# The last stage of layer 0 with residual sums made by accumulating transfers, a pinned instruction order, and first neighbours taken from the chip

## Chip, cores and metric

One core of one Trainium2 chip runs the whole program. The metric is device microseconds of one execution, median of several runs. The engines are named as the profile names them: PE (TensorE), DVE (VectorE), ACT (ScalarE), POOL (GpSimd), SP (SyncE, which here only issues transfers).

## What is computed

Four graph layers over x of shape (8, 2048, 64), with an adjacency of 2048 x 2048. The change touches the end of layer 0 and the start of layer 1:

```python
# layer 0: industry = (adj/deg) @ (h W_ind); g = hypergraph attention
def attn_scores(f):
    return jnp.tanh(f @ fcW + fcb) @ av
pair   = jnp.stack([industry, g], axis=2)
coefs2 = jax.nn.softmax(attn_scores(pair), axis=-1)
out    = jnp.einsum('bnk,bnkf->bnf', coefs2, pair)
x = x + out
# layer 1
h = jnp.maximum(_layernorm(x), 0.0) @ W
e = leaky_relu(s_src[:, :, None] + s_dst[:, None, :], 0.2)
x = x + elu(softmax(where(adj > 0.5, e, -inf)) @ h)
```

A softmax over two entries is a sigmoid of the difference of the scores, and sigmoid(d) is (1 + tanh(d/2))/2. So with c = tanh((s_ind - s_g)/2) the layer adds g + 0.5 (1 + c)(industry - g) to x.

## The kernel before

Two of the eight batches sit side by side on the 128 partitions (64 features each), so there are NP = 4 pairs p. The 2048 nodes of a pair are cut into NCW = 4 pieces c of CW = 512 columns. A chunk is one (p, c), a tile of 128 x 512 fp32 or 256 KB; there are 16.

Layer 0 first computes `industry` and writes it to DRAM (`ind_dram`, line 947), then g, which stays on the chip in `gT` (four tiles of 128 x 2048, the same memory as `hn`; last written by line 1165). Then comes the stage that the change rewrites, lines 1193 to 1264. For each chunk:

- `front` (1211): load `iv` from `ind_dram` on SP; `scores` twice, for `iv` and for the columns of `gT`: two matmuls with `fcW` into `pf` (1206) and one tanh of 128 x 1024 on ACT into `th_s` (1208); on DVE the difference of the two `th_s` (1217) and `iv - gv` (1218).
- `back` (1221): two matmuls with `Av` into `pd` (1224), tanh on ACT into `cc` (1226), and three DVE operations (1227, 1228, 1229) that end in x + out; the tile goes to `x1_dram` by a transfer that POOL issues (1230).
- `inputs` (1232): x of the chunk, `xo`, is loaded on SP into one of five buffers.

`back` runs two chunks behind `front`. After the last chunk of a pair, `late_tile` (1827) loads 1 MB of the adjacency over `gT[p]`, from POOL's queue.

Between chunks the generator `neighbour_steps(0)` of layer 1 (1288) is advanced, from the eighth chunk on: for each c it loads x1 of pair 0 back from `x1_dram` (1302), takes the layer norm (`mean`, `var`, Square, Ln, Exp: lines 730 to 741), and multiplies by `W1x` into `ph` (1319), from which `vd`, `sc` and `hS` are made (1320 to 1322). At its end it makes `wd` and `rs` (1328, 1330), transposes `rs` and writes it to `r_dram` (1337). For the first half of pair 0, the broadcast rows R are built on the chip: 8 small matmuls into `pb` (1345) and 4 ACT copies (1346).

Then `attend` of layer 1 starts: for each of 16 tiles m, DVE makes two `pt` (1387) from R, `wd` and the adjacency, and PE multiplies them into `o` and `dn`. This loop is PE's from then on.

The order of instructions on an engine is chosen by a scheduler except where `keep_in_program_order` pins it; in this stage only every second matmul of a pair is pinned (1198). A transfer waits in its issuing engine's queue (SP or POOL) until what it needs is there, and everything behind it in that queue waits too. Transfers issued by SP run on the queue that the profile calls q1, those issued by POOL on q0.

Of the kernel before, what the change touches and what calls it, by code (L numbers as in the profile page):

```python
# [8 lines left out]
FP = mybir.dt.float32  # L9
FR = mybir.dt.float32r  # L10
AF = mybir.ActivationFunctionType
OP = mybir.AluOpType
# [4 lines left out]
P = 128  # L17
# [601 lines left out]
LN_EXP = "natural_log_exp_and_others"  # L619


class Kit:


# [124 lines left out]
def layer0(kit, hn, x1_dram, open_early, late_tile, between):  # L749
# [40 lines left out]
    with ExitStack() as sA:  # L790
# [110 lines left out]
        with ExitStack() as s1:  # L901
# [11 lines left out]
            def industry(c):  # L913

                acc = [ps.tile([P, CW], FP, tag=f"acc{p}", name=f"acc{p}") for p in range(NP)]
                ds = sb.tile([P, 2, CW], FR, tag="ds", name="ds")
                for g in range(NT // 2):
                    at = sp.tile([P, 2, CW], FR, tag="at", name="at")
                    nc.gpsimd.dma_start(
                        out=at,  # L920
                        in_=t["adjT"][g * 2 * P : (g + 1) * 2 * P, cols(c)].bitcast(FR).rearrange("(k p) n -> p k n", p=P),
                    )
                    for k in range(2):
                        m = 2 * g + k
                        for p in range(NP):
                            for h in range(2):
                                mm(acc[p], Y[h][:, m, p, :], at[:, k, :], start=m + h == 0, stop=m == NT - 1 and h == 1)  # L927
                        if units:
                            units.pop(0)()

                    if g > 0:
                        nc.vector.tensor_tensor(ds, (was if g == 1 else ds).bitcast(FP), at.bitcast(FP), op=OP.add)
                    was = at
                ev = [sb.tile([P, CW], FP, tag="ev", name="ev", bufs=4) for p in range(NP)]
                for p in range(NP):
                    (nc.scalar.copy if p % 2 else nc.vector.tensor_copy)(ev[p], acc[p])  # L936
                deg = ps.tile([P, CW], FP, tag="ph", name="deg", bufs=2)
                for k in range(2):
                    mm(deg, ones_r, ds[:, k, :], start=k == 0, stop=k == 1)
                rdeg = sb.tile([P, CW], FP, tag="rdeg", name="rdeg", bufs=1)  # L940
                nc.vector.tensor_reduce(bad[:, 3 + c : 4 + c], deg, AX.X, OP.min)
                nc.vector.tensor_scalar(bad[:, 3 + c : 4 + c], bad[:, 3 + c : 4 + c], 0.5, None, op0=OP.is_lt)
                nc.vector.tensor_scalar_max(rdeg, deg, 1.0)
                nc.vector.reciprocal(rdeg, rdeg)
                for p in range(NP):
                    nc.vector.tensor_mul(ev[p], ev[p], rdeg)
                    nc.sync.dma_start(out=ind_dram[p, :, cols(c)], in_=ev[p])
# [152 lines left out]
    with ExitStack() as s0:  # L1100
# [64 lines left out]
                nc.scalar.activation(gT[p][:, i * P : (i + 1) * P], pt[:, p, :], AF.Identity, bias=neg1)  # L1165

        now = begin(0)
        late = None
        for i in range(NT):
            pg = ps.tile([P, B, F], FP, tag="pg", name="pgs")  # L1170
# [16 lines left out]
        late()  # L1187

    sP.close()
    next_ = between(None)  # L1190


    with ExitStack() as s0:
        io = s0.enter_context(tc.tile_pool(name="o_io", bufs=7, reuse_waits="tile"))
        sb = s0.enter_context(tc.tile_pool(name="o_sb", bufs=2, reuse_waits="tile"))
        ps = s0.enter_context(tc.tile_pool(name="o_ps", bufs=2, space=PSUM, reuse_waits="tile"))

        def pinned(ins, first):

            if not first:  # L1200
                tc.keep_in_program_order(ins)

        def scores(v):
            pf = ps.tile([P, 2, CW], FP, tag="pf", name="pf")
            for b2 in range(2):
                pinned(mm(pf[:, b2, :], fcW[half(b2), :], v[half(b2), :], start=True, stop=True), b2 == 0)
            th = sb.tile([P, 2, CW], FP, tag="th", name="th_s", bufs=4)
            nc.scalar.activation(th, pf, AF.Tanh, bias=fcb)
            return th

        def front(p, c):
            s = cols(c)
            iv = io.tile([P, CW], FP, tag="iv", name="iv")
            nc.sync.dma_start(out=iv, in_=ind_dram[p, :, s])
            gv = gT[p][:, s]
            th = [scores(iv), scores(gv)]
            nc.vector.tensor_sub(th[0], th[0], th[1])
            nc.vector.tensor_sub(iv, iv, gv)
            return p, s, gv, th[0], iv

        def back(x, p, s, gv, th, df):
            pd = ps.tile([P, CW], FP, tag="pd", name="pd")
            for b2 in range(2):
                pinned(mm(pd[half(b2), :], Av, th[:, b2], start=True, stop=True), b2 == 0)
            cc = sb.tile([P, CW], FP, tag="cc", name="cc", bufs=1)
            nc.scalar.activation(cc, pd, AF.Tanh, scale=0.5)
            nc.vector.scalar_tensor_tensor(df, cc, 1.0, df, op0=OP.add, op1=OP.mult)
            nc.vector.scalar_tensor_tensor(df, df, 0.5, gv, op0=OP.mult, op1=OP.add)
            nc.vector.tensor_add(x, x, df)
            nc.gpsimd.dma_start(out=x1_dram[p, :, s], in_=x)  # L1230

        def inputs(p, c):
            x = sb.tile([P, CW], FP, tag="x", name="xo", bufs=5)
            nc.sync.dma_start(out=x, in_=t["xT"][p, :, cols(c)])
            return x

        behind, freed, xs = [], [], []

        def finish():
            p, c, rest = behind.pop(0)  # L1240
            back(xs.pop(0), *rest)
            if freed:
                late_tile(freed.pop())
            if c == NCW - 1:
                freed.append(p)

        for p in range(NP):
            for c in range(NCW):
                behind.append((p, c, front(p, c)))
                if len(behind) > 1:  # L1250
                    xs.append(inputs(*behind[-2][0:2]))

                if NCW + 2 < p * NCW + c:
                    next(next_, None)
                if len(behind) > 2:
                    finish()
                if NCW + 2 < p * NCW + c:
                    next(next_, None)
        xs.append(inputs(*behind[-1][0:2]))
        for _ in next_:  # L1260
            pass
        while behind:
            finish()
        late_tile(freed.pop())
    ctx.close()


class Layer1:
# [19 lines left out]
    def neighbour_steps(self, p):  # L1288
# [3 lines left out]
        nc, mm = kit.nc, kit.mm  # L1292
        x1_dram, r_dram = self.x1_dram, self.r_dram

        keep = self.sb2 if p else sb
        sc = sb.tile([P, NT, 4], FP, tag="sc", name="sc", bufs=1)
        vd = keep.tile([P, NT, 2], FP, tag="vd", name="vd", bufs=1 + (p > 0))
        wd = keep.tile([P, NT, 2], FP, tag="wd", name="wd", bufs=1 + (p > 0))
        hS = None
        for c in range(NCW):  # L1300
            x = sb.tile([P, CW], FP, tag="x", name="x1", bufs=1)
# [27 lines left out]
        rs = sb.tile([P, 2, NT], FP, tag="rs", name="rs", bufs=1)  # L1329
        nc.scalar.activation(rs, sc[:, :, 2:4].rearrange("p t b -> p b t"), AF.Exp, scale=-0.8)  # L1330
        pr = ps.tile([2 * NT, P], FP, tag="h", name="pr")
        one = nc.tensor.transpose(pr, rs.rearrange("p b t -> p (b t)"), kit.ident)
        if kit.strict:
            kit.tc.keep_in_program_order(one)
        rr = sb.tile([2 * NT, P], FP, tag="rr", name="rr", bufs=1)
        nc.vector.tensor_copy(rr, pr)
        nc.sync.dma_start(out=r_dram[p].rearrange("b (t n) -> (b t) n", n=P), in_=rr)
        self.first = [self.scores(p, 0, b2) for b2 in range(2)] if p == 0 else None

        for b2, r in enumerate(self.first or ()):  # L1340
            for k in range(2):
                pb = ps.tile([P, 4, P], FP, tag=("ln", "h")[k], name="pb1")
                for j in range(4):
                    one = rs[:, b2, 4 * k + j : 4 * k + j + 1]
                    mm(pb[:, j, :], one.to_broadcast([P, P]), kit.ident, start=True, stop=True)
                nc.scalar.copy(r[:, cols(k)], pb.rearrange("p k n -> p (k n)"))
        yield hS, vd, wd

    def scores(self, p, hf, b2):

        self.turn += 1
        r = (self.sb2 if self.turn % 3 == 0 else self.R).tile([P, HN], FP, tag="R", name="R", bufs=2 - (self.turn % 3 == 0))
        if p == hf == 0:
            return r
        self.kit.nc.sync.dma_start(out=r, in_=self.r_dram[p, b2 : b2 + 1, cols(hf, HN)].to_broadcast([P, HN]))
        return r

# [57 lines left out]

        return [lambda: total(0), end]

    def run(self, aT, now, following):

# [4 lines left out]
        self.ps2 = l1.enter_context(tc.tile_pool(name="att_ps", bufs=2, space=PSUM, reuse_waits="tile"))  # L1426
        kit.use_ln_exp()
        kit.strict = True
        ends = []
        for p in range(NP):  # L1430
            last = p == NP - 1
            if last:
# [362 lines left out]
def four_layers(  # L1795
# [13 lines left out]
    with ExitStack() as s:  # L1809
# [18 lines left out]
            load(NT - NP + p, low.tile([P, N], FR, tag=f"hn{p}", name=f"aTl{p}"))  # L1828

        def between(_):  # L1830
            one = Layer1(kit, x1)
            ahead.append(one)

            def steps():
                for r in one.neighbour_steps(0):
                    yield
                ahead.append(r)

            return steps()

        layer0(kit, hn, x1, early, late_tile, between)
        later = []
# [2 lines left out]
            later.append(Layers23(kit, x1, x3, out, part, ctx))  # L1845
            return later[0].front(ps)

        ahead[0].run(aT, ahead[1], following)
        later[0].run(aT)
        ps = s.enter_context(tc.tile_pool(name="flag_ps", bufs=1, space=PSUM))  # L1850
        nc.vector.tensor_reduce(kit.bad[:, 0:1], kit.bad, AX.X, OP.add)
# [47 lines left out]
```

## Time and profile before

| what | us |
|---|---|
| runs before, median (lowest to highest) | 2101.84 (2101.09 to 2102.75) |
| the profiled execution, its own time | 2095.15 |
| its span | 2093.3 |
| last transposes of g (line 1163) start | 436.14 |
| first matmul of the stage (line 1206) | 437.16 |
| `wd`, `rs` on ACT | 523.36 to 523.73 |
| first two `pt` of layer 1 start on DVE | 532.94 and 534.15 |
| first `o` matmul | 534.27 |

The stage takes 97 us, from 437 to 534, a twentieth of the span; the 1560 us after it are bound by PE and the change does not touch their instructions. A line of the timeline reads: start, duration, engine, line, operation, output<-inputs, shapes, count; the bracket is the idle time before it and what ended it. In a chain of waits each row is start, duration, and what the end was waiting for in that time.

### The profile page before, as it was taken

How to read it: one execution, taken by the hardware profiler on the slowest of the kernel's cores; microseconds unless marked ns; L12 is line 12 of the kernel's file. 1: busy time of each engine (PE TensorE's matmuls, PEld its weight loads, DVE VectorE, ACT ScalarE, POOL GpSimd, SP SyncE). 2: the span in 40 equal slices, each digit the busy share in tenths (PEclk: the TensorE clock that was granted, in tenths of full speed). 3: DMA queues.
4: the chain of work that ended last, by engine and by line, in shares of the span. 5: the costliest groups of instructions: out<-in, count | busy, mean ns of one | idle time of the engine just before them, and what ended most of it. 6: DMA issues, size and time to landing. Idle time of an engine off the chain costs nothing.

```text
span 2093.3 us, 23652 instructions
## 1 busy us (share of the span) xinstructions
PE 2017.3 (96%) x9164; PEld 1153.1 (55%) x9164; DVE 1211.8 (58%) x1906; ACT 461.6 (22%) x863; POOL 260.1 (12%) x384
## 2 busy tenths in 40 slices
PE   7999998988999999999999999999999999999997
PEld 4777655622332223226776457765477755577653
DVE  6677388876888888884223652226642246522355
ACT  4321244456211111112121111211111211112100
POOL 0211054420000000000001120002110012100022
PEclk9999899998999999999999999999999999999999
DMA  5666272145211111213210112101022001121000
GB/s 128 184 193 194 81 254 53 37 138 163 63 40 43 39 44 23 61 31 81 59 46 16 28 28 66 56 11 31 22 59 62 30 21 25 37 66 56 6 16 12
DMA packets 85001, 136.06 MB, mean 65 GB/s; under 512 B 32912, under 2 KB 33168, under 8 KB 82640
## 3 DMA queue, kind: packets, MB, share of 16 engines
q1 hardware_dynamic: 66832, 83.86, 13.8%
q0 software_dynamic: 18048, 50.60, 8.8%
q8 instruction: 74, 1.21, 0.2%
q14 instruction: 47, 0.39, 0.1%
HBM read 103.69 MB, written 30.74 MB: 64 GB/s over the span
## 4 chain that ended last, share of the span: by engine, by line
PE 68%; issue 15%; DVE 6%; POOL 5%; DMA 3%; ACT 2%; POOLq 0%; SPq 0%; DVEq 0%; ACTq 0%
PE acc L713 27%; PE o L713 11%; PE dn L713 6%; PE u L713 6%; PE acc L927 2%; PE pgs L1155 2%; PE var L713 2%; PE mean L713 2%; PE py L713 2%; POOL fold L1780 1%; DVE ex L1153 1%; PE ph L713 1%; POOL ot L1781 1%; DMA at<-in_adjT 1%; POOL mix L1154 1%
## 5 line engine op out<-in xcount | busy, mean ns | idle before, releaser
L713 PE MATMUL acc<-aT,parts 128*128 128x512 f32 x1664 | 456.0, 420 | 0.0
L713 PEld LDWEIGHTS acc<-aT,parts 128*128 128x128 f32 x1664 | 307.8, 188 | 111.8 <-issue 49.4
L1768 DVE TENSOR_TENSOR pr<-u,embf 128x512 f32<-128x512 f32 x256 | 170.5, 686 | 139.0 <-PE u L713 132.3
L1387 DVE SCALAR_TENSOR_TENSOR pt<-R,wd,aT 128x1024 f32<-128x1024 f32 x192 | 236.6, 1277 | 22.2 <-PE dn L713 8.4
L713 PE MATMUL o<-pt,hS 128*64 128x512 f32 x1024 | 239.4, 604 | 6.5 <-DVE pt L1387 6.5
L713 PE MATMUL u<-W3f,y 64*128 64x512 f32 x1024 | 241.0, 589 | 0.0
L713 PEld LDWEIGHTS u<-W3f,y 64*128 64x128 f32 x1024 | 99.2, 187 | 120.6 <-issue 120.6
L713 PEld LDWEIGHTS o<-pt,hS 128*64 128x64 f32 x1024 | 68.7, 137 | 166.9 <-issue 151.3
L713 PE MATMUL u<-W3f,v 64*128 64x512 f32 x512 | 138.8, 619 | 0.0
L927 PE MATMUL acc<-at,Y 128*128 128x512 f32 x512 | 134.8, 408 | 1.5 <-DVE ev L936 1.5
L713 PE MATMUL dn<-pt,vd 128*32 128x512 f32 x1024 | 123.1, 598 | 0.0
L1604 DVE TENSOR_TENSOR yb<-py,cb_f 128x512 f32<-128x512 f32 x32 | 22.1, 691 | 173.8 <-PE py L713 173.8
L1780 POOL TENSOR_TENSOR fold<-fold 128x256 f32<-128x256 f32 x64 | 47.7, 746 | 548.5 <-DVE fold L1779 510.6
L927 PEld LDWEIGHTS acc<-at,Y 128*128 128x128 f32 x512 | 93.9, 191 | 24.5 <-issue 4.3
L713 PE MATMUL acc<-aTl,parts 128*128 128x512 f32 x384 | 103.1, 405 | 0.0
L1772 DVE TENSOR_TENSOR pr<-pr 128x512 f32<-128x512 f32 x128 | 88.0, 688 | 2.2
L1387 DVE SCALAR_TENSOR_TENSOR pt<-R,wd,aTl 128x1024 f32<-128x1024 f32 x64 | 79.7, 1281 | 11.5 <-PE dn L713 8.2
L713 PEld LDWEIGHTS acc<-aTl,parts 128*128 128x128 f32 x384 | 72.2, 188 | 21.5 <-issue 5.7
L1155 PE MATMUL pgs<-mix,S 128*128 128x512 f32 x128 | 69.7, 635 | 12.8 <-POOL mix L1154 12.0
L1754 ACT COPY xs<-px 128x128 f32<-128x128 f32 x64 | 17.1, 267 | 272.7 <-POOL ot L1782 210.2
L1154 POOL TENSOR_TENSOR mix<-ex,wt 128x512 f32<-128x512 f32 x64 | 66.6, 1042 | 74.1 <-DVE ex L1153 65.0
L1672 POOL TENSOR_TENSOR bq<-bq,xp 128x512 f32<-128x512 f32 x16 | 20.5, 1282 | 434.1 <-DVE xp L1670 395.6
(307 smaller groups left out, 2709.1 us busy)
## 6 DMA issues: line engine op xcount, KB each, us to landing
at<-in_adjT POOLq DMA_DIRECT2D x32, 512.0 KB, 4.6
raw<-in_adjT SPq DMA_DIRECT2D x64, 256.0 KB, 3.3
aT<-in_adjT POOLq DMA_DIRECT2D x12, 1024.0 KB, 5.9
xp<-xd SPq DMA_DIRECT2D x45, 256.0 KB, 2.9
R<-r_dram SPq DMA_DIRECT2D x14, 512.0 KB, 3.9
hi_dram<-hi SPq DMA_DIRECT2D x16, 264.0 KB, 2.5
lo_dram<-lo SPq DMA_DIRECT2D x16, 264.0 KB, 3.4
hhi<-hi_dram POOLq DMA_DIRECT2D x16, 264.0 KB, 3.0
```

Source lines behind the costliest of these rows:

```text
L713: one = self.nc.tensor.matmul(*args, **kw)
L927: mm(acc[p], Y[h][:, m, p, :], at[:, k, :], start=m + h == 0, stop=m == NT - 1 and h == 1)
L1153: nc.vector.scalar_tensor_tensor(ex, mix, 1.0, ex, op0=OP.max, op1=OP.min)
L1154: nc.gpsimd.tensor_tensor(mix, ex, wt[:, k, :, None].to_broadcast([P, B, F]), op=OP.mult)
L1155: return lambda: mm(flat(pg), S[:, k, :], flat(mix), start=k == 0, stop=k == NB - 1)
L1387: nc.vector.scalar_tensor_tensor(pt, R[b2], wd[:, m, b2 : b2 + 1], aT[m][:, s].bitcast(FP), op0=OP.max, op1=OP.mult)
L1604: nc.vector.tensor_tensor(yb, py, bias[:, None, :].to_broadcast([P, 4, P]), op=OP.add)
L1672: nc.gpsimd.tensor_add(bq, bq, xp)
L1768: nc.vector.tensor_tensor(a, u[h], emb[:, i, 8 * w : 8 * w + 8, None].to_broadcast([P, 8, F]), op=OP.mult)
L1772: nc.vector.tensor_add(pr[h], pr[h], a)
L1780: nc.gpsimd.tensor_add(fold[:, :, 0:2, :], fold[:, :, 0:2, :], fold[:, :, 2:4, :])
L1781: nc.gpsimd.tensor_add(ot, fold[:, :, 0, :], fold[:, :, 1, :])
```

## The change

The stage becomes a software pipeline in a fixed order: all its matmuls, ACT and DVE instructions are pinned (`InOrder` wraps an engine and pins all that it issues). At step i the engines get `first(i+1)` (load, scores of industry), `second(i+1)` (scores of g, and `iv - gv/2`), `third(i-1)` (`pd` and its tanh, now written in place in PSUM), `differ(i)` and `fourth(i-2)`.

The arithmetic is rearranged. `ind_dram` now holds half of industry (the reciprocal of twice the degree), and the tanh of its scores has scale 2. `fourth` makes df = (1 + c)(ind/2 - g/2) in one operation. What is left, x + g + df, is summed differently by pair: for pair 0 on DVE, with x loaded into four tiles `xs` that stay on the chip; for pairs 1 to 3 in DRAM: x is copied there from the input early (three transfers of 1 MB, DRAM to DRAM, issued by SP), `gT[p]` is added to it by a transfer with `accum_op=add` (1 MB each, POOL), and each chunk's df by another (256 KB each, POOL).

`first_neighbours` replaces `neighbour_steps(0)`: it works on two pieces at a time, straight from `xs`, and is advanced twice a step from step 4 on. R of the first half is now loaded from `r_dram` (two transfers of 512 KB) and no longer built from `pb`.

```diff
-                nc.vector.tensor_scalar_max(rdeg, deg, 1.0)
+                nc.vector.tensor_scalar(rdeg, deg, 1.0, 2.0, op0=OP.max, op1=OP.mult)
...
         now = begin(0)
+        for p in range(1, NP):
+            nc.sync.dma_start(out=x1_dram[p], in_=t["xT"][p])
...
+    V, A = InOrder(tc, nc.vector), InOrder(tc, nc.scalar)
+        io = s0.enter_context(tc.tile_pool(name="o_io", bufs=9, reuse_waits="tile"))
...
+        def first(i):
+            p, c = chunks[i]
+            iv = ivs[i] = io.tile([P, CW], FP, tag="iv", name="iv")
+            nc.sync.dma_start(out=iv, in_=ind_dram[p, :, cols(c)])
+            ths[i] = scores(iv, 2.0)
+        def second(i):
+            p, c = chunks[i]
+            tgs[i] = scores(gT[p][:, cols(c)], 1.0)
+            V.scalar_tensor_tensor(ivs[i], gT[p][:, cols(c)], -0.5, ivs[i], op0=OP.mult, op1=OP.add)
+        def differ(i):
+            V.tensor_sub(ths[i], ths[i], tgs.pop(i))
+        def third(i):
+            pd = ps.tile([P, CW], FP, tag="pd", name="pd")
+            th = ths.pop(i)
+            for b2 in range(2):
+                mm(pd[half(b2), :], Av, th[:, b2], start=True, stop=True)
+            A.activation(pd, pd, AF.Tanh, scale=0.5)
+            ccs[i] = pd
+        def fourth(i):
+            p, c = chunks[i]
+            df = ivs.pop(i)
+            V.scalar_tensor_tensor(df, ccs.pop(i), 1.0, df, op0=OP.add, op1=OP.mult)
+            if p:
+                nc.gpsimd.dma_start(out=x1_dram[p, :, cols(c)], in_=df, accum_op=OP.add)
+            else:
+                V.tensor_add(df, df, gT[p][:, cols(c)])
+                V.tensor_add(xs[c], xs[c], df)
+                nc.sync.dma_start(out=x1_dram[p, :, cols(c)], in_=xs[c])
+            if c == NCW - 1:
+                late_tile(p)
...
+        for i in range(len(chunks) + 2):
+            if i > 3:
+                next(steps, None)
+            if 0 < i < len(chunks) - 1:
+                first(i + 1)
+            if i < len(chunks) - 1:
+                second(i + 1)
+            if 0 < i <= len(chunks):
+                third(i - 1)
+            if i < len(chunks):
+                differ(i)
+            if i > 1:
+                fourth(i - 2)
+            if i > 3:
+                next(steps, None)
+            if i in (1, 4, 8):
+                p = 1 + i // 4
+                nc.gpsimd.dma_start(out=x1_dram[p], in_=gT[p], accum_op=OP.add)
...
+    def first_neighbours(self, xs, V, A):
...
+        for d in (0, 2):
...
+            mean = [ps.tile([P, CW], FP, tag=g, name="mean") for g in ("ln", "h")]
+            for k in range(2):
+                mm(mean[k], kit.avg, xs[d + k], start=True, stop=True)
+            yield
+            for k in range(2):
+                V.tensor_sub(xc[k], xs[d + k], mean[k])
+            yield
+            for k in range(2):
+                A.activation(q[k], xc[k], AF.Square)
+            yield
+            var = [ps.tile([P, CW], FP, tag=g, name="var") for g in ("ln", "h")]
+            for k in range(2):
+                mm(var[k], kit.avg, q[k], start=True, stop=True)
+            yield
+            for k in range(2):
+                A.activation(q[k], var[k], AF.Ln, bias=kit.eps)
+            for k in range(2):
+                A.activation(q[k], q[k], AF.Exp, scale=-0.5)
+            yield
+            for k in range(2):
+                V.scalar_tensor_tensor(xc[k], xc[k], 0.0, q[k], op0=OP.max, op1=OP.mult)
+            yield
...
+            for k in range(2):
+                two = []
+                for g in range(2):
+                    m = 4 * (d + k) + 2 * g
+                    ph = ps.tile([P, 2, P + 4], FP, tag=("ln", "h")[g], name="ph")
+                    for j in range(2):
+                        at = (2 * g + j) * P
+                        mm(ph[:, j, :], xc[k][:, at : at + P], kit.W1x, start=True, stop=True)
+                    two.append((slice(m, m + 2), ph))
+                yield
+                for ms, ph in two:
+                    A.activation(vd[:, ms, :], ph[:, :, P : P + 2], AF.Exp, scale=0.2)
+                for ms, ph in two:
+                    V.tensor_copy(sc[:, ms, :], ph[:, :, P:])
+                    V.tensor_tensor(
+                        hS[:, ms, :].rearrange("p t (b f) -> p t b f", b=2),
+                        ph[:, :, 0:P].rearrange("p t (b f) -> p t b f", b=2),
+                        vd[:, ms, :, None].to_broadcast([P, 2, 2, F]), op=OP.mult,
+                    )
+                yield
+        A.activation(wd, sc[:, :, 0:2], AF.Exp, scale=0.8)
+        rs = sb.tile([P, 2, NT], FP, tag="rs", name="rs", bufs=1)
+        A.activation(rs, sc[:, :, 2:4].rearrange("p t b -> p b t"), AF.Exp, scale=-0.8)
+        yield
+        pr = ps.tile([2 * NT, P], FP, tag="h", name="pr")
+        kit.turn(pr, rs.rearrange("p b t -> p (b t)"))
+        rr = sb.tile([2 * NT, P], FP, tag="rr", name="rr", bufs=1)
+        V.tensor_copy(rr, pr)
+        nc.sync.dma_start(out=self.r_dram[0].rearrange("b (t n) -> (b t) n", n=P), in_=rr)
+        self.first = [self.scores(0, 0, b2) for b2 in range(2)]
...
     def scores(self, p, hf, b2):
-        if p == hf == 0:
-            return r
```

In the built program the scheduler, which is free for transfers, has put the three copies of x into SP's queue right behind the last loads of x (before: issued at 40 to 42 us), and the three accumulates of `gT` one behind the other at the head of the stage in POOL's queue, ahead of the late tiles and of all accumulates of df. POOL's order from there is: `gT` 1, 2, 3; late tiles 0 and 1; df of pair 1; late tile 2; df of pair 2; late tile 3; df of pair 3. SP's is: `iv` 0 and 1; the four `xs`; `iv` 2 to 8; then the four stores of x1 of pair 0 among `iv` 9 to 12; `iv` 13 to 15; one load of x1 of pair 1; `r_dram`; R.

## Prediction

> **What bounds the kernel now.** I read the page, then busy times by stretch, the chain of waits, and the timelines of PE, DVE and ACT, all for the stage from 437 to 534 us.
>
> ```profile
> PE 2017.3 (96%) x9164; PEld 1153.1 (55%) x9164; DVE 1211.8 (58%) x1906; ACT 461.6 (22%) x863; POOL 260.1 (12%) x384
> ...
> xd<-e POOLq DMA_DIRECT2D x8, 512.0 KB, 5.5
> ```
> ```profile
> 429.00:436.00 7.00, 3.77 (x5) 0.80 (x4) 3.40 (x4) 0.84 (x2) 2.08 (x2) 0.73 0.16 58
> 436.00:533.00 97.00, 81.51 (x277) 28.72 (x277) 68.17 (x106) 65.97 (x87) 9.85 (x19) 0.90 0.52 164
> 471.00:477.00 6.00, 0.04 (x2) 0.00 (x0) 0.00 (x0) 2.85 (x4) 0.00 (x0) 0.68 0.72 255
> 477.00:487.00 10.00, 9.74 (x18) 3.41 (x18) 4.09 (x7) 1.38 (x3) 0.00 (x0) 0.51 0.23 71
> ```
>
> PE bounds the program (first line); in this stage it does not do so alone. The columns of the second block are length, PE, weight loads, DVE, ACT, POOL, granted clock, transfer share, GB/s. From 471 to 477 PE did nothing, and for the next 10 us it ran at half clock (0.51), so some 6.2 + 5 = 11 us of the 97 are one stall. The chain says what it was:
>
> ```profile
> 461.93 0.50 POOL aTl L1820
> 462.46 10.04 DMA xd<-xo
> 472.51 0.33 SPq L1234
> 472.94 4.19 DMA x<-xd
> 477.26 2.04 PE mean L713 x2
> ```
>
> A store of x1 stood behind the 1 MB late tile in POOL's queue and took 10.04 us; SP waited for its buffer, and the load that the first neighbours need stood behind that. Outside the stall the pace is this (PE, DVE, ACT):
>
> ```profile
> 446.88 1.13 PE L1206 MATMUL pf<-iv,fcWf 64*128 64x512 f32 x4
> ...
> 449.80 1.13 PE L1206 MATMUL pf<-iv,fcWf 64*128 64x512 f32 x4
> ```
> ```profile
> 450.93 1.22 DVE L1217 TENSOR_TENSOR th_s<-th_s 128x1024 f32<-128x1024 f32 x1
> 452.06 0.68 DVE L1227 SCALAR_TENSOR_TENSOR iv<-cc,iv 128x512 f32<-128x512 f32 x1
> 452.67 0.68 DVE L1218 TENSOR_TENSOR iv<-iv,hn 128x512 f32<-128x512 f32 x1
> ...
> 454.59 1.22 DVE L1217 TENSOR_TENSOR th_s<-th_s 128x1024 f32<-128x1024 f32 x1
> ```
> ```profile
> 512.83 1.28 ACT L739 ACT_TABLE_LOAD   x1 [0.44 <-PE var L713]
> 514.13 0.69 ACT L739 ACTIVATE q<-var,eps_f 128x512 f32<-128x512 f32 x1
> 514.83 1.28 ACT L1208 ACT_TABLE_LOAD   x1
> ```
>
> A chunk takes PE 2.92 us (446.88 to 449.80). DVE needs 3.66 for its five operations (450.93 to 454.59), and from 450 to 462 DVE is on the chain. With first neighbours between, a piece c costs ACT two table loads.
>
> **The change, part by part.** I follow the stage to the start of layer 1's second `pt` (534.15 before), because `o` needs two.
>
> *DVE.* Starts are 1.13 apart after the wide subtraction and 0.61 after the others, so pairs 1 to 3 need 1.13 + 2 x 0.61 = 2.4 us a chunk and pair 0 about 3.7 (two more additions, each 0.11 later because it needs the one before). 12 x 1.2 = 15 us of DVE go; that is worth only what brings a step down from 3.66 to PE's 2.92.
>
> *PE to the end of step 1.* The same matmuls as before 446.88, at the same half clock: step 2 starts at 447.
>
> *Steps 2 to 13.* 12 x 2.92 = 35.0. Into them go 4 `mean` and 4 `var` at 1.06 (start to start, 489.23 to 490.29) and 8 `ph` groups at 0.64: 8.5 + 5.1 = 13.6. Since all orders are pinned, PE also waits:
> - 2.1 + 0.6 us for the first `mean` and `var`: x of chunk 1 is the last of pair 0's 3.7 us on DVE.
> - 3.2 and 2.3 us at the first `ph` of each half: Ln and Exp of two pieces hold ACT for 2 x 1.28 + 2 x 0.60 + 2 x 0.53 = 4.8 us with the next tanhs behind them, and PE has one chunk of work to cover it.
> - 3 x 1.6 us where a `ph` or `mean` takes the PSUM of the `ph` before it: in order come the tanh of `pd` 0.59, two `vd` 0.3, two `sc` and `hS` 0.84.
>
> That is 13.0. Handoffs between engines cost 0.04 to 0.3 in the timelines; I add 2 for the lot. Step 14 starts at 447 + 35.0 + 13.6 + 13.0 + 2 = 510.6, and `rs` ends 2.4 later (two `hS`, two exponentials): 513.0, against 523.73.
>
> The tanh into PSUM and DVE's read of it have no row of their own; the nearest are the tanh into SBUF (0.59) and DVE's PSUM read of line 1148 (0.68). I take those; 0.1 either way would be hidden by PE.
>
> *The stall.* x of pair 0 no longer goes through DRAM, and nothing in the stage waits for a store of x1 except `iv` 13 to 15, which need the accumulates of chunks 4 to 6 landed. Those are issued by about 480 and wanted after 500. So this stall goes; what is late next is the following.
>
> *The three accumulates of `gT`.* POOL issues 3 MB at 438, one behind the other. The row above: 512 KB take 5.5 us to land; the one issued at 609.10 kept q0 busy for 59.9% of the stretch 609 to 615, 3.6 us. So 3 MB hold q0 from 440 to about 461 (6 x 3.6). Loads of `iv` are on q1 beside it. A row for such company is the late tile at 464 to 467:
>
> ```profile
> q0 software_dynamic: 121, 0.81, 82.9%
> q1 hardware_dynamic: 3, 0.00, 0.4%
> ```
>
> q0 moved 0.81 MB, q1 next to nothing with loads waiting. `iv` 0 to 3 and the four `xs` should be in by 441; `iv` 4 is due on PE at 450, and another every 3 us. Bounds: 0 if q1 gets a chunk in between every few us; 10 if nothing comes before 461. I take 2, nearer the lower end, because at 469 to 471 the same two queues shared (0.56 MB on q1, 0.17 on q0).
>
> [...] No row here has 3 MB on q0 in a row.
>
> *The clock.* PE's waits of 2 to 3 us may halve it. A wait of 2.19 us at 429 to 431 was enough for that (clock 0.73 in the first stretch, 0.50 after to 442), and one of 2.0 us at 465 was not. Four of the new waits are about as long. Bounds 0 and 6.8 (twice 6.8 us at half clock); I take 3.
>
> [...]
>
> *R from DRAM.* 32 matmul records of `pb` (4.05 us of PE) and 4 copies go. In their place, after `rs`: transpose and copy of `rr` 2.1 (behind `pd` on PE and three operations on DVE), `r_dram` 1.5, issue 0.35, R 3.9, the second R 1.7 behind it (512 KB at some 300 GB/s), and 0.9 because late tile 3 and df of pair 3 go out at the same time (0 to 3): 10.45. Before, from `rs` to the second `pt`: 10.4. So this is even. The last two `third` and `fourth` (7 us) lie beside it.
>
> *Copies of x, DRAM to DRAM.* 3 MB on q1 from 42 us. Stretch 50 to 60 moved nothing before (0 GB/s); the next adjacency loads go out at 60.85. At 200 to 300 GB/s they need 10 to 15 us and end by then: 0, at worst 4.
>
> *Late tiles* leave a little earlier and are wanted 80 us later: 0. `ind` halved, scale 2: same instructions, 0.
>
> **Sum.** `rs` at 513.0 + 2 + 3 = 518.0; second `pt` at 528.5 against 534.15: 5.7 us less. The profiled execution, 2095.15, would be 2089.4. The runs' median, 2101.84, is 6.7 above that execution; a stage's gain should come off it unchanged: 2096.1.
>
> **Rivals.**
> - *Clean*: no half clock, no late load, R undisturbed, so the terms 2, 3 and 0.9 fall away: gain 5.7 + 5.9 = 11.6, 2090. For it: the first mechanism of the stall is really gone. Against it: PE waits of 3 us are in the order itself.
> - *Paid back*: half clock twice (6.8 in place of 3) and R behind late tile and accumulates (3 in place of 0.9): 5.9 worse than the sum, gain -0.2, 2102. For it: 0.51 at 477 to 487; against it: q0 is short of work by then.
> - *Starved*, the slow side: `gT`'s accumulates keep q1 shut until 461. Step 3 stands from 450 for 10 us (8 more than taken), and PE comes back at half clock as at 477 to 487 (5 lost): 5.7 - 8 - 5 = -7.3, 2109. From a delay of 7 us on it decides (5.7 + 2 - 7 - 5 = -4.3). For it: the 0.4% row. Against it: the sharing at 469 to 471, and three transfers have gaps.
>
> **Chances.** Likeliest, own range 2093 to 2099: 0.46. Clean 0.17, paid back 0.20, starved 0.17. Differences under 0.2% (4.2 us) can't be told from no change here (the runs span 1.7). Most of the likeliest and all of clean are faster: 0.53; the rest of the likeliest and paid back: 0.29; starved and a little more: 0.18. The range takes in all but the ends of clean and of starved: 2089 to 2107.
>
> **What would show it.** Right: no PE wait above 3.5 us in the stage, `rs` 3 to 9 us earlier, `rs` to second `pt` within 2 us of 10.4, q0 busy without a break from 440 to 461. Wrong: a wait of PE `pf` on `iv` near 450 (starved), granted clock below 0.85 over the stage with no such wait (paid back), adjacency loads waiting at 61 us, or any move after 540.

## The result and the profile after

Eight runs of each on one chip: the changed kernel 2094.43 us (2089.18 to 2097.95), the kernel before 2099.18 (2088.54 to 2102.75), ratio 0.9983 with a 95% interval of 0.9960 to 1.0006: no difference that these runs can tell. (A ratio is estimated from all runs of both kernels, so it is not exactly that of the two medians.) A second set of runs on another chip, 12 and 23 of them, gave 2093.61 against 2094.32, ratio 1.0001 (0.9986 to 1.0015). The profiled execution took 2096.54 (span 2094.7; before 2093.3).

So the stall went and the time hardly moved. To see where it went I measure from the stage's first matmul, which starts 3.6 us later in this profile than in the one before (440.76 against 437.16; why is told under the hardware):

| us | before | after |
|---|---|---|
| first `pf` to `rs` | 86.6 | 76.4 |
| `rs` to second `pt` | 10.4 | 18.4 |
| first `pf` to second `pt` | 97.0 | 94.9 |
| first `pf` to the second `mean` inside layer 1's loop | 117.4 | 116.4 |

The stage won 10.2 us up to `rs`, gave 8.0 back before layer 1 could start, and 1.1 more behind that, where PE was still at half clock (0.52 from 535.6 to 542). The page's busy line, which answers to the one of before:

```profile
PE 2006.4 (96%) x9132; PEld 1151.8 (55%) x9132; DVE 1196.8 (57%) x1882; ACT 453.1 (22%) x855; POOL 264.3 (13%) x383
...
L1473 DVE SCALAR_TENSOR_TENSOR pt<-R,wd,aT 128x1024 f32<-128x1024 f32 x192 | 236.6, 1279 | 29.5 <-DMA R<-r_dram 14.0
```

PE has 11 us less to do, DVE 15, ACT 8.5: the work did shrink as foretold. The new row is the second: `pt` now waits for R, 14.0 us in all. The median landing of all 16 loads of R, 4.0 us on the page, hides the ones that matter.

Busy times by stretch (length, PE, weight loads, DVE, ACT, POOL, clock, transfer share, GB/s), from the first `pf` to `rs` and then a part of the end:

```profile
440.80:517.20 76.40, 62.68 (x231) 22.55 (x232) 47.46 (x74) 52.41 (x74) 11.17 (x14) 0.92 0.75 184
...
525.00:535.00 10.00, 0.00 (x0) 0.00 (x0) 0.61 (x1) 0.37 (x1) 0.84 (x1) 0.50 1.00 223
```

In the first stretch PE is busy 82%; from 525 to 535 it does nothing while the transfer engines are full. The chain of waits names the two links, and POOL's and SP's timelines the company they had (first block the chain: start, duration, what; second the two issues, start and duration first):

```profile
519.63 6.48 DMA r_dram<-rr
526.12 8.12 DMA R<-r_dram
...
534.38 1.29 DVE pt L1473
```
```profile
518.24 0.56 POOL L1906 DMA_DIRECT2D aTl<-in_adjT  x1 [1.23 <-PE pd L726]
...
519.63 0.32 SPq L1432 DMA_DIRECT2D r_dram<-rr  x1
```

A store of 16 KB took 6.48 us. It was issued 1.39 us after late tile 3, 1 MB. In the kernel before the order was the other way round:

```profile
524.94 0.33 SPq L1337 DMA_DIRECT2D r_dram<-rr  x1
...
532.94 0.54 POOL L1820 DMA_DIRECT2D aTl<-in_adjT  x1 [3.05 <-DVE iv L1228]
```

There the store went first by 8.00 us and landed in 1.4. The change frees `gT[3]` earlier, since its last reader is now `second(15)` and no longer the last `back`; so the late tile overtook the store. During the store's 6.5 us the queues moved this (packets, MB, share of the 16 engines):

```profile
q0 software_dynamic: 411, 1.50, 92.1%
q1 hardware_dynamic: 48, 0.02, 1.2%
```

None of the store's 48 packets on q1 had moved by 523. All of them moved from 523 to 526, 43 in the first of these microseconds:

```profile
q1 hardware_dynamic: 48, 0.02, 2.6%
```

The late tile landed 7.7 us after its issue, at 525.9, and the store 0.2 later. So the store did not move slowly: it stood until the load ahead of it was nearly through.

### The profile page after: what moved, and what is told of

Same layout as the page of the kernel before. It is cut to its first block, busy times and chain, and to the rows that moved or that the text cites. A ratio compares the mean times of both kernels' runs of the same rounds, so it can differ in the third digit from the quotient of the medians.

```text
span 2094.7 us, 23522 instructions
## 1 busy us (share of the span) xinstructions
PE 2006.4 (96%) x9132; PEld 1151.8 (55%) x9132; DVE 1196.8 (57%) x1882; ACT 453.1 (22%) x855; POOL 264.3 (13%) x383
## 4 chain that ended last, share of the span: by engine, by line
PE 57%; issue 12%; POOL 3%; DVE 2%; DMA 1%; ACT 1%; POOLq 0%; DVEq 0%; SPq 0%; ACTq 0%
PE acc L726 27%; PE o L726 11%; PE u L726 6%; PE dn L726 5%; PE py L726 2%; PE mean L726 2%; PE var L726 1%; POOL fold L1866 1%; POOL ot L1867 1%; POOL ot L1868 1%; PE ph L726 1%; DMA R<-r_dram 1%; PE prd L726 1%; PE tp L732 1%; PE pv L726 1%
## 5 line engine op out<-in xcount | busy, mean ns | idle before, releaser
L726 PE MATMUL o<-pt,hS 128*64 128x512 f32 x1024 | 238.2, 602 | 13.7 <-DVE pt L1473 13.5
L1169 PE MATMUL pgs<-mix,S 128*128 128x512 f32 x128 | 69.7, 635 | 13.0 <-POOL mix L1168 12.4
L1168 POOL TENSOR_TENSOR mix<-ex,wt 128x512 f32<-128x512 f32 x64 | 66.6, 1042 | 76.7 <-DVE ex L1167 66.3
```

Source lines behind the costliest of these rows:

```text
L726: one = self.nc.tensor.matmul(*args, **kw)
L1168: nc.gpsimd.tensor_tensor(mix, ex, wt[:, k, :, None].to_broadcast([P, B, F]), op=OP.mult)
L1169: return lambda: mm(flat(pg), S[:, k, :], flat(mix), start=k == 0, stop=k == NB - 1)
```

## The experiments

Each row is one profile, except for the time and its ratio. "Start" is the first `pf`; the last column runs to the second `mean` in layer 1's loop, past all that the stage disturbs.

| run | median, us (one: a single run) | ratio to before (95%) | start | to `rs` | store of `r_dram` | `rs` to 2nd `pt` | to 2nd `mean` |
|---|---|---|---|---|---|---|---|
| before | 2099.18 | | 437.16 | 86.6 | 1.4 | 10.4 | 117.4 |
| changed | 2094.43 | 0.9983 (0.9960-1.0006) | 440.76 | 76.4 | 6.5 | 18.4 | 116.4 |
| e1 late tile 3 held | 2089.81 | 0.9976 (0.9964-0.9989) | 444.51 | 75.7 | 1.5 | 11.7 | 107.6 |
| e2 quiet | 2085.98, one | | 437.40 | 75.8 | 1.5 | 12.3 | 109.5 |
| e3 R on the chip | 2086.60 | 0.9963 (0.9948-0.9979) | 437.49 | 75.7 | 6.4 | 9.8 | 107.2 |
| e4 three steps | 2083.36 | 0.9945 (0.9930-0.9960) | 441.10 | 68.2 | 6.1 | 16.2 | 108.3 |
| e5 before, late tiles held | 2085.20 | 0.9963 (0.9947-0.9978) | 438.57 | 77.4 | 1.4 | 10.4 | 107.8 |
| e6 two R | 2086.89, one | | 439.11 | 76.4 | 1.5 | 11.6 | 108.3 |
| e7 no `gT` accumulate | 2111.36, one | | 445.13 | 82.0 | 6.4 | 22.7 | 126.4 |
| e8 spread | 2087.36 | 0.9960 (0.9944-0.9975) | 444.35 | 66.3 | 2.6 | 17.5 | 105.6 |
| e9 three, held | 2084.13 | 0.9939 (0.9919-0.9959) | 436.19 | 68.2 | 6.4 | 16.2 | 106.1 |
| e10 R on the chip, held | 2085.86 | 0.9945 (0.9924-0.9965) | 435.86 | 75.7 | 1.7 | 9.8 | 106.4 |
| e11 changed again | 2093.61 | 1.0001 (0.9986-1.0015) | 437.85 | 76.7 | 6.6 | 17.8 | 114.7 |
| e12 e1 again | 2089.39 | 0.9978 (0.9964-0.9991) | 436.58 | 78.5 | 1.5 | 14.3 | 113.8 |

e1 to e4 shared a chip and its runs of the kernel before (median 2094.93), e5 to e8 another (2093.77), as did e9 and e10 (2097.86) and e11 and e12 (2094.32).

**e1, late tile 3 held.** The theory at this point: late tile 3 and the accumulates of df, on q0, slow the store and the loads of R on q1.

```diff
         def late_tile(p):
+            if p == NP - 1:
+                a = low.tile([P, N], FR, tag=f"hn{p}", name=f"aTl{p}")
+                nc.gpsimd.tensor_copy(a[:, 0:2], ahead[0].first[1][:, 0:2])
+                return load(NT - NP + p, a)
...
-            if c == NCW - 1:
+            if c == NCW - 1 and p < NP - 1:
                 late_tile(p)
...
         for _ in steps:
             pass
+        late_tile(NP - 1)
```

> Late tile 3 waits until R of the first half is in; the four df accumulates of pair 3 go out as before. If the queue of late tile and accumulates (2 MB on q0 from 518 to 529) is what slows r_dram and R: the store of r_dram lands about 2 to 4 us sooner, rs to the second pt 13 to 15 us in place of 18.4, because 1 MB of accumulates is still there; time 3 to 5 us less than the changed kernel. If the round trip of R through DRAM costs 18 us by itself: no change within 1 us in that stretch. If the half clock is what eats the gain: stretch unchanged too.

The chain of waits of e1:

```profile
522.71 1.48 DMA r_dram<-rr
524.20 5.88 DMA R<-r_dram
```

The store is 5.0 us shorter, more than expected, with the accumulates still there; `rs` to second `pt` 11.7, under the 13 to 15 expected. So it was the late tile that held the store, and not the accumulates.

**e2, quiet.** On top of e1:

```diff
-            if p:
+            if p == NP - 1 and c:
+                pass
+            elif p:
                 nc.gpsimd.dma_start(out=x1_dram[p, :, cols(c)], in_=df, accum_op=OP.add)
```

> As before it, and the accumulates of df for the last three chunks of pair 3 are left out, so that part of x1 lacks df (chunks 13 to 15) and q0 is nearly empty while R is fetched. Queue theory: r_dram lands 1.5 us after its issue and R some 4 us after its own, rs to the second pt 10 to 11 us, as the prediction had it (10.45 less 0.9). Round trip by itself: 17 us or more. The stretch from the first pf to rs should not move (76.4 us, within 2).

The store took 1.50, but R 6.68 (its row in the chain), not some 4, so the end stayed at 12.3: 2 us of the working were wrong even with q0 nearly empty. The accumulates of the last chunks cost nothing that shows (12.3 here, 11.7 with them).

**e3, R of the first half on the chip.**

```diff
         self.first = [self.scores(0, 0, b2) for b2 in range(2)]
+        for b2, r in enumerate(self.first):
+            for k in range(2):
+                pb = ps.tile([P, 4, P], FP, tag=("ln", "h")[k], name="pb1")
+                for j in range(4):
+                    one = rs[:, b2, 4 * k + j : 4 * k + j + 1]
+                    mm(pb[:, j, :], one.to_broadcast([P, P]), kit.ident, start=True, stop=True)
+                A.copy(r[:, cols(k)], pb.rearrange("p k n -> p (k n)"))
```

with `scores` returning the empty tile for p = hf = 0, as before.

> R of the first half of pair 0 is built on the chip from rs with the 16 matmuls into pb and 4 ACT copies, as in the kernel before; all else is the changed kernel. Queue theory, where the loss is the trip through DRAM: rs to the second pt 8 to 10.5 us (8 matmul groups about 4 us, copies 0.6 each, two chunks' ends between), 8 to 10 us less than the changed kernel in that stretch, and about that in the whole time. Half-clock theory: the clock after the idle 12.4 us of PE was half until 542; with the idle time gone the second half of this (6 us) is won as well or, if it has another cause, stays.

9.8 us, inside the range; the store still stood 6.4 us behind late tile 3, and nobody waited for it. Of PE's 12.4 idle us ahead of the first `o` 2.6 remained, and from that `o` to the first `dn` it was 5.8 us (523.17 to 528.93) in place of 6.4 (535.82 to 542.18, in the changed kernel's 20.5 us of half clock: 0.50 from 521.4 to 541.9). The time fell to a ratio of 0.9963. What was late next is in DVE's timeline of e3:

```profile
530.35 2.48 DVE L1482 SCALAR_TENSOR_TENSOR pt<-R,wd,aT 128x1024 f32<-128x1024 f32 x2 [3.65 <-DMA xd<-iv]
```

The fifth `pt` waits for memory that accumulates of df are still reading.

**e4, three steps.** `next(steps, None)` once more, ahead of `third`, from i = 5 on; nothing else.

```diff
+            if i > 4:
+                next(steps, None)
             if 0 < i <= len(chunks):
                 third(i - 1)
```

> The steps of the first neighbours are advanced three times a step of the stage in place of twice, so that rs is done some four steps (12 us) earlier and R comes from DRAM while chunks 12 to 15 are still computed. Queue theory with the trip hidden: the second pt starts when the last chunk's matmuls are through, 523 to 527 in place of 535.6 with a stage start at 440.76; 8 to 12 us less. Rival, waits: less work between dependent steps makes the PE waits for Ln and Exp longer (3.4 and 2.5 us would be 4 to 5 each) and halves the clock more often; gain 2 to 6 us only.

`rs` came 8 us earlier, R was in before it was wanted, and the second `pt` started 84.4 us after the first `pf` in place of 94.9: 10.5 less, in the range. The waits did grow (4.01 at the first `ph`), as the rival said, but its price was too high. Ratio 0.9945.

**e5, the kernel before with late tiles held.** This asks what the rewrite was needed for.

```diff
         def late_tile(p):
-            load(NT - NP + p, low.tile([P, N], FR, tag=f"hn{p}", name=f"aTl{p}"))
+            a = low.tile([P, N], FR, tag=f"hn{p}", name=f"aTl{p}")
+            tc.keep_in_program_order(nc.gpsimd.tensor_copy(a[:, 0:2], ahead[1][2][:, 0, :]))
+            load(NT - NP + p, a)
...
-            if freed:
-                late_tile(freed.pop())
-            if c == NCW - 1:
-                freed.append(p)
...
-        late_tile(freed.pop())
+        for p in range(NP):
+            late_tile(p)
```

and the stores of x1 pinned, so that the late tiles stay behind them.

> The kernel before, with one edit: all four late tiles are held until wd of pair 0 is made, so no 1 MB load stands on q0 while x1 is stored and read back. If the stall of 471 to 487 was the store behind the late tile, as the prediction says: the idle 6.2 us and the half clock after it (5 us) go, first pf to second pt 86 to 90 us in place of 97.0, and the time falls by 7 to 11 us, about what the whole rewrite was forecast to bring. Rival, DVE as the next bound (3.66 us a chunk against PE's 2.92): only 3 to 5 us. Rival, other causes of the wait: no change within 2.

The stage in e5, and the stretch in which PE had stood still:

```profile
437.40:525.40 88.00, 77.10 (x277) 27.45 (x277) 68.28 (x107) 66.00 (x87) 8.19 (x15) 0.96 0.47 145
472.00:478.00 6.00, 4.58 (x16) 1.61 (x14) 2.42 (x3) 4.13 (x7) 0.00 (x0) 1.00 0.72 231
```

The same 277 matmul records in 88.0 us in place of 97.0, clock 0.96 in place of 0.90; first `pf` to second `pt` 87.8, 9.2 less. The median fell by 8.6 us (2093.77 to 2085.20), as expected. Its ratio, 0.9963, is that of e3 and better than the changed kernel's. The first reading of the stall is shown right, and so is that it could be had by moving four loads.

**e6, two R.** e2, and the third load of R held by a copy from the first R on POOL.

```diff
+        if p == 0 and hf == 1 and b2 == 0:
+            self.kit.nc.gpsimd.tensor_copy(r[:, 0:2], self.held[:, 0:2])
+        if p == hf == 0:
+            self.held = r
```

> The kernel of e2 (late tile 3 held, df of chunks 13 to 15 left out), and the third load of R, which is for the second half of the nodes, held until the first is in. Sharing theory (three loads of 512 KB on q1 at once): the first R lands 3.9 to 4.5 us after its issue in place of 6.65, the second 5.6 to 6.5, rs to the second pt about 10.5 in place of 12.25. If the transfers go one after the other in any case: first and second R as in e2, within 0.3.

Missed: the first R took 6.32 (chain) and the second was there 1.2 later at the latest. The third load was not what slowed them. Whether two loads at once share, or the first one pays for the single accumulate beside it, stays open: one R alone took 3.9 in the kernel before and 4.2 in e5, but 6.6 in e3, with the accumulates of pair 3 on q0 (81.1% busy from 515 to 530).

**e7, `gT` added on DVE.** The three accumulates of `gT` go, `V.tensor_add(df, df, gT[p][:, cols(c)])` comes.

```diff
             if p:
+                V.tensor_add(df, df, gT[p][:, cols(c)])
                 nc.gpsimd.dma_start(out=x1_dram[p, :, cols(c)], in_=df, accum_op=OP.add)
...
-            if i in (1, 4, 8):
-                p = 1 + i // 4
-                nc.gpsimd.dma_start(out=x1_dram[p], in_=gT[p], accum_op=OP.add)
```

> The three 1 MB accumulates of gT are left out and gT is added on DVE in one more operation a chunk for pairs 1 to 3 (0.61 us start to start, 12 of them). If the accumulates cost what the trace says (one wait of 0.96 us on iv): first pf to rs within 1.5 us of 76, nothing lost on DVE, which has 2.4 + 0.6 against PE's 2.92. If they do slow the stage: 2 us or more less. End of the stage (rs to second pt 18.4) unchanged.

Missed by far: 5.6 us more to `rs`, 4.3 more behind it, the slowest kernel of all. Two waits of DVE, at the first `pt` and at the second, show the second part:

```profile
546.13 1.28 DVE L1471 SCALAR_TENSOR_TENSOR pt<-R,wd,aT 128x1024 f32<-128x1024 f32 x1 [10.03 <-DMA xd<-iv]
549.80 6.07 DVE L1471 SCALAR_TENSOR_TENSOR pt<-R,wd,aT 128x1024 f32<-128x1024 f32 x5 [2.39 <-DMA R<-r_dram]
```

With `gT` read by `fourth`, late tile 2 left POOL at 528.06 (497.58 in the changed kernel), ahead of the last accumulates, and late tile 3 at 536.95, 0.25 us after the first load of R. So 2 MB moved beside the accumulates and the loads of R; the second R, on which the second `pt` waited, landed 12.7 us after its issue. The first part adds up, as an estimate from PE's timeline and the granted clock (0.86 from 445 to 527 here, 0.92 from 440.8 to 517.2 in the changed kernel): 22.4 us at half clock between the first `pf` and `rs` in place of 12.3, so 5.1 lost more; PE's waits for `hS` and `xc` 1.4 longer together; the wait of 0.96 for `iv` gone: 5.5. Not all of the half clock comes from DVE's added work: 3.3 us more of it (5.3 in place of 2.0, so 1.6 of the 5.1 lost) lie at the start of the stage, ahead of the first added operation: the first 8 `pf` of `iv` took 3.79 us here and 2.97 in the changed kernel. In this order of the queues the accumulates pay for themselves; `gT` added on DVE with the late tiles held was not run.

**e8, spread.** Three steps as in e4, one after `first`, one after `second`, one at the end of the step.

```diff
-            if i > 3:
-                next(steps, None)
             if 0 < i < len(chunks) - 1:
                 first(i + 1)
+            if i > 3:
+                next(steps, None)
             if i < len(chunks) - 1:
                 second(i + 1)
+            if i > 3:
+                next(steps, None)
```

> As e4, three steps of the first neighbours in each step of the stage, but spread: one after first, one after second, one at the end, so that one matmul group of 1 to 2 us lies between dependent steps. If PE's waits come from too little work between: the sum of PE's waits from the first mean to rs falls from e4's 12.2 us to 6 to 9 and the stretch from the first pf to the second pt from 84.35 to 79 to 82. If the waits are set by the length of the chain on ACT (Ln and Exp of two pieces 4.8 us): within 2 us of e4.

PE's timeline of e8:

```profile
476.20 2.13 PE L726 MATMUL ph<-W1x,xc 128*128 128x132 f32 x8 [4.39 <-DVE xc L630]
...
501.06 2.13 PE L726 MATMUL ph<-W1x,xc 128*128 128x132 f32 x8 [4.01 <-DVE xc L630]
```

83.8 us to the second `pt` against e4's 84.4, within the 2 us of the second theory. PE's waits from the first `mean` to `rs` add up to 12.6 us against e4's 12.2, where the first theory had 6 to 9: it is refuted. That ACT's chain of Ln and Exp sets the waits is what is left, but not shown by itself, since in e4 the second of the two waits was 1.34. The 1.9 us less to `rs` go with less half clock: 12.2 us of it in place of 19.0, an estimate from the lengths of the matmuls in the two timelines (8 `ph` 2.10 to 2.13 us long where the clock was half and 1.14 to 1.17 elsewhere).

**e9, three steps with late tile 3 held**, behind all accumulates of df (e4 and e1 together, accumulates and copy pinned on POOL).

```diff
-                nc.gpsimd.dma_start(out=x1_dram[p, :, cols(c)], in_=df, accum_op=OP.add)
+                tc.keep_in_program_order(nc.gpsimd.dma_start(out=x1_dram[p, :, cols(c)], in_=df, accum_op=OP.add))
```

> e4 (three steps of the first neighbours in each step of the stage) with late tile 3 held, as in e1, and put behind all df accumulates of pair 3. e4's next loss was the fourth pt, which waited 4.29 us for accumulates that stood behind late tile 3. If that is the same queue effect: this wait falls under 1 us, dn's wait of 1.5 us and the half clock of 3.4 us after it go, 2 to 3.5 us less than e4 from the first pf to 545 us, some 2 us in the time. The store of r_dram still stands behind late tile 2 (6 us), hidden. Rival: the accumulates themselves are late, no change within 1 us.

DVE's timeline of e4, then of e9:

```profile
526.92 1.29 DVE L1475 SCALAR_TENSOR_TENSOR pt<-R,wd,aT 128x1024 f32<-128x1024 f32 x1 [0.23 <-DMA xd<-iv]
532.50 1.28 DVE L1475 SCALAR_TENSOR_TENSOR pt<-R,wd,aT 128x1024 f32<-128x1024 f32 x1 [4.29 <-DMA xd<-iv]
535.05 2.48 DVE L1475 SCALAR_TENSOR_TENSOR pt<-R,wd,aT 128x1024 f32<-128x1024 f32 x2 [1.27 <-DMA xd<-iv]
```
```profile
522.78 1.28 DVE L1476 SCALAR_TENSOR_TENSOR pt<-R,wd,aT 128x1024 f32<-128x1024 f32 x1 [1.01 <-DMA xd<-iv]
525.37 1.28 DVE L1476 SCALAR_TENSOR_TENSOR pt<-R,wd,aT 128x1024 f32<-128x1024 f32 x1 [1.31 <-DMA xd<-iv]
527.93 2.48 DVE L1476 SCALAR_TENSOR_TENSOR pt<-R,wd,aT 128x1024 f32<-128x1024 f32 x2 [1.27 <-DMA xd<-iv]
```

The wait of the fourth `pt` fell from 4.29 to 1.31, not under 1, that of the third rose from 0.23 to 1.01, and that of the fifth stayed at 1.27. `dn` waited no more. It is 2.2 us less to the second `mean`, within what was expected, but the 16 `o` behind the first `dn` took 4.70 us in both (3.65 in the next group), and the accumulates are late by themselves too (the last landed 8.1 us after its issue). In the time e9 (0.9939) and e4 (0.9945) can't be told apart. With e10 they have the lowest ratios, some 0.6% below the kernel before.

**e10, R on the chip with late tile 3 held** (e3 and e1 together, with e9's pins; two steps, not three).

> e3 (R of the first half built on the chip) with late tile 3 held behind the df accumulates and the R that is built. If late tile 3 is all that disturbs the end of the stage: first pf to second pt as in e3 (85.6, within 1), the wait of 3.65 us of the fifth pt on accumulates goes, and the time is 0 to 3 us below e3's. Against e1 (late tile held, R through DRAM, 87.5) the stretch stays 1 to 3 us shorter.

85.6 to the second `pt`, as expected; the wait on accumulates shrank from 3.65 to 1.56 and did not go. The ratio, 0.9945, can't be told from e3's 0.9963: the intervals overlap.

**e11 and e12, the changed kernel and e1 on one chip,** because their first times came from different chips.

> The changed kernel once more, beside e1's kernel on one chip, because its first times came from another chip than e1's. Queue theory: the store of r_dram stands behind late tile 3 in this profile too (6 us or more), rs to second pt 17 to 20 us, first pf to the second mean of layer 1 some 116 us; its ratio to the kernel before stays at 0.996 to 1.000.

> e1 once more, beside the changed kernel. Queue theory: store of r_dram 1.5 us, rs to second pt 11.5 to 12.5, first pf to the second mean 107 to 109, and its median 5 to 9 us below the changed kernel's of the same call. If the stretch at the end is given back later in the program: the medians within 2 us of each other although the stretch is shorter.

The store behaved as before in both, 6.6 against 1.5 us. The medians of 12 runs each differ by 4.2 us (2093.61, 2089.39): just under the 5 to 9 expected, and more than the 2 of its rival. The means differ by 4.4, with an interval of 1.7 to 7.1 worked out from these runs, so there is a difference, but the rival's 2 is not quite shut out. In the profile of e12 PE waited 4.4 us for `iv` (not at all in e1) and `rs` came 2.8 later; R then took 2.6 us more, for a reason that is not shown, so that its stretch to the second `mean`, 113.8, missed the expected 107 to 109. It is only 0.9 shorter than e11's 114.7, so this pair of profiles does not show where the 4.2 us come from. The changed kernel's ratio, 1.0001, is just above the 0.996 to 1.000 expected. Holding one load wins back some 4 us of the time; the single profile of e1 made it look like 9.

The waits for `iv` in PE's timeline of e11:

```profile
445.09 1.13 PE L726 MATMUL pf<-iv,fcWf 64*128 64x512 f32 x4 [2.76 <-DMA iv<-ind_dram]
...
452.42 1.13 PE L726 MATMUL pf<-iv,fcWf 64*128 64x512 f32 x4 [1.40 <-DMA iv<-ind_dram]
```

## Why the prediction held in its number and not in its sum

The forecast of 2096.1 us was 1.7 above the median, inside its own range of 2093 to 2099. But it said 5.7 us faster, and the two sets of runs say 4.7 and 0.7, both with an interval that holds no change at all; the profile shows 2.1 of the 5.7 at the second `pt`. That the number held is in part luck: `rs` came 4.4 us sooner than the sum had it and the end took 8.0 longer, and the kernel before, over eight runs, has a median 2.7 below the 2101.84 from which the forecast set out. By its steps:

- *The stall of 471 to 487 as the thing to win*: right, shown by e5 alone (9.2 us of the stage).
- *To `rs`*, 80.8 us from the first `pf` (518.0 - 437.16): 76.4, and 75.7 to 76.7 in e1, e2, e3, e6, e10 and e11. Too high by 4.4. Its PE waits of 13.0 were 12.4 (1.98, 3.37, 1.41, 1.55, 2.50, 1.56, each at a place that was forecast; the 0.6 at `var` did not come). Too dear were the matmuls between (`mean` and `var` 0.94 and not 1.06, a `ph` group 0.53 and not 0.64: 11.8 in place of 13.6), the handoffs (0.8, what is left of the 65.1 us of steps 2 to 13, in place of 2), the accumulates of `gT` (0.96 in place of 2) and the start of the stage, where 2.0 us were at half clock and not 5.2.
- *The accumulates of `gT`*: bounds 0 to 10, taken 2; measured 0.96 in this profile and 4.2 and 4.4 in e11 and e12. Starved, the slow rival, was real in kind and never near its price. q0 did stay full to 460 (89.0% from 455 on), and q1 still got this, from 450 to 455:

```profile
q0 software_dynamic: 130, 0.93, 89.7%
q1 hardware_dynamic: 130, 0.24, 14.3%
```

  That is a chunk of 256 KB in 5 us, against one wanted every 2.93: the loads issued ahead carried PE over. Each queue moved 130 packets.
- *The clock*: taken 3, bounds 0 to 6.8. Half clock at 460.0, 477.0 and 504.3 (granted 0.52, 0.51 and 0.51), 3.4 us each up to `rs`: 5.1 us lost. Within the bounds, 2.1 above the value.
- *`rs` to second `pt`*, 10.45: 18.4. This is the step that failed, and its words were "0.9 because late tile 3 and df of pair 3 go out at the same time (0 to 3)" and "Late tiles leave a little earlier and are wanted 80 us later: 0". What counted was not when the late tile is wanted but what is issued just behind it: 5.0 us of the 8.0 are the store, 1.4 (6.8 in e2, 8.3 here) the loads of R in the same company, the rest R itself, priced by a load that was alone (3.9) where two or three went out together (6.3 to 6.7 in the chains of e2 and e6). The row with the right price stood in the prediction's own first part: a store that took 10.04 us behind a late tile. It was used for the stall that goes and not for the store that comes.
- *Copies of x*: 0, as said. The next adjacency loads went out at 61.05 against 60.85 before, and e2, e3, e9 and e10, which have the copies too, start the stage at 435.9 to 437.5 (the kernel before: 437.2).
- *Rivals*: paid back is what happened, by its mechanism (R behind late tile and accumulates), with 6.2 us (18.4 against e2's 12.3) where it had 3, and with a cheaper stage that made up for some of it. The chance of 0.20 was too low: the condition for it, late tile first, could be read from the order of the instructions.

## What to carry to other kernels

When an edit frees a buffer earlier, look at which bulk load starts then, and which small transfer of the critical path is issued on another queue before that load has landed (7.7 us in the changed kernel). Here a store of 16 KB behind a load of 1 MB took 6.1 to 6.6 us in six profiles and 2.6 in a seventh, against 1.4 to 1.7 without the load; as an estimate from the six, price the small one at what is left of the large one. Try the one-line move before the rewrite: holding four loads in the old kernel (0.9963) brought, as far as the intervals tell, as much as any repair of the new one (0.9939 to 0.9976). And read a change of half a percent from a fixed anchor in the profile to another, over several profiles, and then confirm it in the time on one chip, since e1's 9 us were 4 in the median.

## What the runs showed of the hardware

A 16 KB store took 1.4 to 1.7 us with no late tile just ahead of it (seven profiles), 6.1 to 6.6 when a 1 MB load had been issued on the other queue 1.4 to 2.3 us before (changed, e3, e4, e7, e9, e11), and 2.6 when it had been 2.8 us before (e8). In the six it landed 7.8 to 8.7 us after the load's issue, in e8 5.4. In the changed kernel the load landed 7.7 us after its issue and the store 0.2 after that.

In the profiles of the kernel before and of the changed one the granted clock was 0.50 in stretches of 3.4, 6.8, 10.2, 13.7 and 20.5 us (10.2 from 432.2 and 13.7 from 473.1 before, 6.8 from 111.8 and 20.5 from 521.4 after), multiples of 3.4; only the stretch that runs to the program's end is of another length. The same wait can be followed by half clock or not. At 110 to 112 us, long before the stage, PE waits for `ev`, 1.5 to 2.9 us in five profiles (before, changed, e2, e4, e5). The clock of the next 7 us in the changed kernel, then in e2:

```profile
112.00:119.00 7.00, 6.62 (x18) 5.28 (x19) 4.99 (x16) 1.17 (x5) 0.00 (x0) 0.53 0.21 80
...
112.38 3.35 PE L940 MATMUL acc<-at,Y 128*128 128x512 f32 x7 [2.88 <-DVE ev L949]
```
```profile
112.00:119.00 7.00, 6.66 (x31) 5.32 (x32) 6.60 (x16) 1.51 (x6) 0.72 (x1) 1.00 0.28 98
...
112.34 2.12 PE L940 MATMUL acc<-at,Y 128*128 128x512 f32 x7 [2.46 <-DVE ev L949]
```

After 2.88 us the clock was halved (0.53), after 2.46 it was not (1.00); after 2.50 it was in e4 (0.76 from 112 to 119), after 2.51 it was not in e5 (1.00 from 111 to 121). Most of the 3.6 us by which the stage began late in the first profile of the changed kernel is lost here: the next `pg` starts at 124.27 against 121.03 before. Between 200 and 260 us, where the two profiles have their half clock at different times, the lag shrinks to 1.1 us (`deg` at 243.16 against 242.02) and grows again. This may be part of why runs of one kernel differ by 6 to 16 us. In the stage of the changed kernel a wait of 1.98 us, up to 459.04, was followed by half clock (0.52 from 460.0 to 463.4), shorter than the 2.46 and 2.51 that were not: in these profiles the length of the wait alone does not tell.
